# A macaron block on one core: weight rows in 1 MB loads by expert pairs n and n + 8, half of the sorted tiles' down matrices addressed on chip, sorted results added in place

## The chip, the cores and the metric

The kernel runs on one core of a Trainium2 chip. The metric is the device time of one execution in microseconds (us); the median of several runs is given, and one further execution was profiled. TensorE is written PE (its weight load PEld), VectorE DVE, ScalarE ACT, GpSimd POOL and SyncE SP, as in the profile.

## The reference

The input x has 8 batches of 1024 tokens with 128 features. Three stages follow each other, each on a layer norm of x and added to x: half of a mixture of experts, causal attention with one head of 128, and half of the same mixture again.

```python
x = x + 0.5 * ffn(layernorm(x))
x = x + attention(layernorm(x))
x = x + 0.5 * ffn(layernorm(x))

# ffn: 16 experts, 64 inner units each, the best 4 per token, and one shared expert
scores = sigmoid(xt @ gate_w.T)
_, idx = top_k(scores + gate_b, 4)
w = scores[idx] / sum(scores[idx]) * 2.5           # comb: w at idx, 0 elsewhere
y = sum over e of comb[:, e, None] * (silu_and_mul(xt @ w13[e].T) @ w2[e].T)
y = y + silu_and_mul(xt @ w13_s.T) @ w2_s.T
```

All is float32.

## The kernel before

**Units of work.** A batch is cut into 8 tiles of 128 tokens, and 4 tiles make a group of 512 (`GT` = 4, `W` = 512). There are 16 groups and two layers of experts, so 32 groups of expert work, done in two ways.

*Dense groups* (class `Group`, 20 of the 32). All 16 experts are computed for all tokens, two experts at a time: the 64 units of two experts fill 128 partitions, so there are `NP` = 8 steps k. Per step PE runs `gate` (L677) and `up` (L683), 128x512 each, ACT the silu (`gate_act`, L690), DVE the product (`units`, L694) into a buffer `hid`, then DVE or POOL multiplies it by the routing weights (`weigh`, L699), and PE adds it to the group's output in PSUM (`down`, L710, four matmuls of 128x128). The shared expert is a ninth term of that sum, and `add` puts it onto x.

The routing weights must lie along the free dimension, the same for all 64 units of an expert. So `store_weights` (L610) writes the transposed weights to DRAM (`cd`, 16 rows of 512), and `load_weights` (L619) reads them back, each row copied to 64 partitions, into buffers `cb`. Before, experts 2n and 2n + 1 form step n; a part has two steps, `CBP` = 4 parts make a group, and each part is loaded by two DMAs of 256 KB, one for either half of the partitions: 8 DMAs a group, 160 in all. Four buffers `cb` exist, so one group's weights.

*Sorted groups* (classes `SortedGroup`, `Chunk`, `Rows`, 12 of the 32, in three chunks of two batches, `CHUNKS`). Only the chosen experts are computed. `sort_steps` normalises, routes, adds the shared expert and puts x away in DRAM (`keep`, L847, into `kept`). `Chunk` numbers the 16 x 128 x 4 (token, expert) pairs by expert, padded to tiles of 128, 80 tiles in all; `scatter` (L1041) writes the normed rows to `rows` in DRAM by indirect DMA on POOL, 64 times a chunk. `rows` exists twice and is cleared to zero beforehand (`clear`, L1516, ten DMAs of 512 KB each). `Rows` then takes 8 tiles at a time as two halves h of 4: `load` (L1112) fetches rows, `turn` (L1143) transposes them on PE, `up` (L1154) multiplies by the expert's gate and up matrices, read from a table on chip at an offset in a register (`find_experts` loads four registers per half on PE), `gate_act`, `units` and `turn_units` (L1178) follow, and `down` (L1187) multiplies by the expert's down matrix: half h = 0 on partitions 0 to 63, half h = 1 on 64 to 127, side by side. The down matrices come from DRAM: `load_down` (L1130, L1136) reads eight offsets into SP's registers and issues eight DMAs of 32 KB into a buffer `wt`, of which there are two. `store` (L1200) writes the result rows. After the chunk, `gather_steps` fetches each tile of `kept` (L864, 64 KB) into a buffer `got`, gathers its four result rows per token by indirect DMA on POOL (L868), adds them with their weights on DVE (L877) and stores the tile (L885), to `kept` in the first layer, to the output in the second. In the first layer x is read again from `kept` later (L1561).

**What sets the order.** No scheduler of the compiler reorders anything: class `Plan` fixes the order of every engine's instructions at build time. Each step has an engine, an expected duration, a rank, the steps it follows, and buffers that it takes and frees. `Plan.run` advances a model clock per engine and each time emits the open step of lowest rank that can begin first. DMAs are issued by SP, whose queue is in order, except the indirect ones on POOL and a few on ACT. A DMA's landing is modelled by one line of transfers at 0.23 MB/us and 1.9 us. Eight semaphores, in turn, mark the landings of SP's and ACT's DMAs. `READY`, `EXPERTS` and so on are base ranks; in `expert_steps` the downs of group p rank at EXPERTS + p - 0.5, before the gates of group p and after those of p - 1.

## Time and profile before

| what | value |
|---|---|
| median of 3 runs | 925.82 us (921.67 to 927.11) |
| the profiled execution, its own time | 927.32 us |
| its span, first to last instruction | 925.5 us |
| mean granted PE clock | 0.987 |
| PE / DVE / POOL / ACT busy | 95% / 74% / 61% / 60% of the span |
| bytes moved by DMA | 139.52 MB, 151 GB/s on the mean |
| queue of SP's DMAs (q1) | 46.0% of 16 engines' span; POOL's indirect ones (q0) 9.7% |
| `cb` loads (L619) | 160 issues, 642 ns of SP each, 103 us together |
| `wt` loads (L1136) | 240 issues, 514 ns of SP each, 123 us together |

How to read it: "busy" is the time in which at least one instruction of the engine runs; "PEclk" and "DMA" are digits for 40 equal slices of the span, a digit being tenths (PEclk: of full speed; DMA: mean busy share of the core's 16 DMA engines). A wait row names the engine and instruction that waited, what ended the wait, and then the total in us, how often, and the longest. Instructions of SP carry the letter q: they issue, and the engine does nothing else. "PE" counts two records for one float32 matmul.

### The profile page before, as it was taken

What the parts mean: (1) busy time and instruction counts of PE and PEld (TensorE: products, weight loads), DVE (VectorE), ACT (ScalarE), POOL (GpSimd) and SP (SyncE); (2) the same over time, 40 slices, a digit from 0 to 9 for tenths busy, and PEclk for the clock granted to TensorE, in tenths of its full rate; (3) what the DMA queues carried; (4) which work ended last, traced back from release to release, by engine and by line L of the source; (5) the groups of instructions that cost most, each with busy time, mean ns of one, the idle gap of its engine ahead of it and who ended that gap; (6) DMA issues with size and microseconds to landing.
All of it is one profiled execution on the core that took longest, in us unless ns stands there. A gap on an engine that the chain in (4) does not pass through costs nothing.

```text
span 925.5 us, 17703 instructions
## 1 busy us (share of the span) xinstructions
PE 882.7 (95%) x5364; PEld 628.9 (68%) x5364; DVE 689.1 (74%) x2194; ACT 555.3 (60%) x1065; POOL 568.5 (61%) x597
## 2 busy tenths in 40 slices
PE   8899999989999999999899999999998989999998
PEld 5547576558587767778677676667576967666665
DVE  5767888848887776877577898687887646687875
ACT  6566644887875566776467567777657535334321
POOL 3442378887446788547475768887865672177560
PEclk9998999999999999999999999999999989999999
DMA  7979661144576844575566543142567567666671
GB/s 218 237 189 246 165 169 37 35 118 127 139 188 173 223 128 125 157 187 141 161 164 153 158 114 116 39 117 68 153 153 191 147 199 202 174 175 170 156 180 35
DMA packets 173694, 139.52 MB, mean 151 GB/s; under 512 B 17760, under 2 KB 144288, under 8 KB 173472
## 3 DMA queue, kind: packets, MB, share of 16 engines
q1 hardware_dynamic: 160032, 111.95, 46.0%
q0 software_dynamic: 12288, 25.19, 9.7%
q10 hardware_dynamic: 1280, 1.26, 0.4%
q8 instruction: 43, 0.70, 0.3%
q14 instruction: 51, 0.42, 0.1%
HBM read 90.49 MB, written 47.84 MB: 149 GB/s over the span
## 4 chain that ended last, share of the span: by engine, by line
PE 58%; POOL 19%; issue 7%; DMA 5%; ACT 4%; DVE 4%; SPq 1%; ACTq 0%; POOLq 0%; DVEq 0%
PE psum L710 13%; POOL rows L1041 12%; PE psum L677 9%; PE psum L683 9%; PE psum L1154 5%; DMA row<-rows 3%; PE psum L1434 3%; PE psum L1143 3%; PE psum L650 3%; PE psum L1187 2%; PE psum L1393 2%; POOL got L868 2%; PE psum L496 2%; PE psum L1421 1%; POOL mv_f L471 1%
## 5 line engine op out<-in xcount | busy, mean ns | idle before, releaser
L868 POOL DMA_INDIRECT got<-results,place x192 | 189.2, 985 | 99.5 <-issue 45.0
L1041 POOL DMA_INDIRECT rows<-xnc,place x192 | 194.8, 1014 | 75.5 <-issue 54.4
L710 PEld LDWEIGHTS psum<-wd,hid 128*128 128x128 f32 x1280 | 159.9, 194 | 33.1 <-issue 20.3
L710 PE MATMUL psum<-wd,hid 128*128 128x128 f32 x1280 | 168.3, 279 | 4.8 <-issue 2.5
L690 ACT ACTIVATE sg<-psum 128x512 f32<-128x512 f32 x160 | 94.5, 597 | 121.6 <-PE psum L677 98.9
L677 PE MATMUL psum<-hT,wg 128*128 128x512 f32 x320 | 164.7, 596 | 1.7 <-ACT sg L690 1.6
L683 PE MATMUL psum<-hT,wu 128*128 128x512 f32 x320 | 163.4, 592 | 0.0
L694 DVE TENSOR_TENSOR hid<-psum,sg 128x512 f32<-128x512 f32 x160 | 109.3, 688 | 56.5 <-PE psum L683 46.9
L683 PEld LDWEIGHTS psum<-hT,wu 128*128 128x128 f32 x320 | 60.8, 190 | 76.5 <-issue 71.5
L699 DVE TENSOR_TENSOR hid<-hid,cb 128x512 f32<-128x512 f32 x132 | 100.7, 770 | 3.0
L1434 PEld LDWEIGHTS psum<-v,prT 128*128 128x128 f32 x576 | 70.1, 192 | 14.3 <-issue 7.8
L1434 PE MATMUL psum<-v,prT 128*128 128x128 f32 x576 | 74.1, 278 | 1.8 <-DVE prT L1425 1.3
L1393 PE MATMUL psum<-k,q 128*128 128x512 f32 (+2 forms) x192 | 71.0, 504 | 3.9 <-POOL k L1310 3.5
L677 PEld LDWEIGHTS psum<-hT,wg 128*128 128x128 f32 x320 | 51.9, 191 | 26.3 <-issue 20.0
L877 DVE SCALAR_TENSOR_TENSOR got<-got,wk 128x128 f32<-128x128 f32 x192 | 65.2, 358 | 3.8 <-DMA got<-results,place 2.1
L1306 POOL TENSOR_TENSOR sg<-sg,cs 128x512 f32<-128x512 f32 x32 | 40.3, 1281 | 44.7 <-ACT sg L1296 44.5
L1154 PE MATMUL psum<-table,hTs 128*128 x480 | 64.3, 282 | 0.1
L1154 PEld LDWEIGHTS psum<-table,hTs 128*128 128x128 f32 x480 | 59.3, 195 | 5.6 <-issue 2.2
L455 DVE BATCH_NORM_STATS2 st<-x 128x6 f32<-128x128 f32 x192 | 53.2, 277 | 11.2 <-DMA x<-in_x 5.1
L1407 ACT ACTIVATE pr<-psum,top 128x128 f32<-128x128 f32 (+3 forms) x64 | 47.5, 745 | 12.1 <-DVE top L1402 11.7
L1425 ACT COPY prT<-psum 128x512 f32<-128x512 f32 (+3 forms) x85 | 37.2, 477 | 27.0 <-PE psum L1421 25.1
L1393 PEld LDWEIGHTS psum<-k,q 128*128 128x128 f32 x192 | 32.8, 196 | 26.3 <-issue 16.1
(148 smaller groups left out, 1515.5 us busy)
## 6 DMA issues: line engine op xcount, KB each, us to landing
cb<-cd SPq DMA_DIRECT2D x160, 256.0 KB
row<-rows SPq DMA_DIRECT2D x60, 256.0 KB
results<-row SPq DMA_DIRECT2D x60, 256.0 KB
rows<-sums SPq DMA_DIRECT2D x20, 512.0 KB
wt<-in_w_down SPq DMA_DIRECT2D x240, 32.0 KB
x<-in_x SPq DMA_DIRECT2D x16, 256.0 KB
kept<-x SPq DMA_DIRECT2D x12, 256.0 KB
rows<-xnc,place POOLq DMA_INDIRECT x192
```

The costliest lines, as they stand in the source:

```text
L677: nc.tensor.matmul(pair_of(("gu", self.id, k))[0], wg[:, k * P : (k + 1) * P], self.hT(), start=True, stop=True,)
L683: nc.tensor.matmul(pair_of(("gu", self.id, k))[1], wu[:, k * P : (k + 1) * P], self.hT(), start=True, stop=True,)
L690: nc.scalar.activation(buf("sg", a), pair_of(a)[0], AF.Silu)
L694: nc.vector.tensor_tensor(buf("hid", a), pair_of(a)[1], buf("sg", a), ALU.mult)
L699: engine.tensor_tensor(hid, hid, cb, ALU.mult)
L710: nc.tensor.matmul(y[:, cols], units[:, cols], wsd if k == NP else wd[:, k, :], start=(self.terms[part] == 1 and j == tiles[0]), stop=(sel ...
L868: nc.gpsimd.indirect_dma_start(out=buf("got", (self.id, j))[:, k, :], out_offset=None, in_=self.chunk.results, in_offset=bass.IndirectOffs ...
L877: nc.vector.scalar_tensor_tensor(got[:, TOPK, :], got[:, k, :], self.chunk.weight[:, self.n * GT + j, k : k + 1], got[:, TOPK, :], ALU.mul ...
L1041: nc.gpsimd.indirect_dma_start(out=row_views[self.n % 2][t * TOPK + k], out_offset=bass.IndirectOffsetOnAxis(ap=self.place[:, t, k : k + 1 ...
L1154: nc.tensor.matmul(p[:, cols], buf("hTs", (self.id, h))[:, cols], table[:, bass.ds(self.at[h][j], D)], start=True, stop=True,)
L1393: nc.tensor.matmul(s[:, c:e], q[:, i * P : self.width], k[:, c:e], start=True, stop=True)
L1434: nc.tensor.matmul(o, buf("prT", self.id)[:, j, :], buf("v", self.b)[:, j, :], start=(j == 0), stop=(j == i),)
```

## The change

- **Routing weights.** Expert n is paired with n + 8 instead of its neighbour, so step n holds experts n and n + 8 (the gate and up matrices are laid out that way by `paired` ahead of the launch, and `wd` is loaded in two halves). `CBP` is 2: a part has four steps, and since the rows of experts n to n + 3 now lie behind each other in `cd`, one DMA of 1 MB loads a part for all 128 partitions. Two buffers `cb` of twice the size.
- **Down matrices of sorted tiles.** A table `low` on partitions 0 to 63 holds the down matrices of all 16 experts (one DMA, `load_low`); half h = 0 of `Rows.down` reads it at the register offset that `up` has loaded. Half h = 1 still loads its four matrices per `Rows`, into the upper partitions of the same tensor, four buffers instead of two.
- **Sorted results.** `gather_steps` fetches a whole group from `kept` into a buffer of `x` (one DMA of 256 KB), adds the gathered rows there and stores the group with one DMA.
- **The planner.** SP's DMAs are modelled on eight lanes, each waiting for its own last landing; `pieces` says how many DMAs a step issues. `PATIENCE` is 3.0; downs rank at + 0.5, after the gates of their own group; early x loads begin at 30, the second clearing of `rows` at 160.
- **Buffers.** `un` and `hs` have one instead of two.

The diff, cut to its core:

```diff
                 work += self.SWITCH
-            self.free_at[e] = end = t + work
+            end = t + work
             if s.port:
                 self.port = end
+            if s.moves and e == "SP":
+                end = t
+                for _ in range(s.pieces):
+                    end = max(end, self.lanes[self.lane]) + work / s.pieces
+                    self.transfers = max(end + 0.5, self.transfers) + s.moves / s.pieces / self.RATE
+                    self.lanes[self.lane] = self.transfers + self.LAND
+                    self.lane = (self.lane + 1) % self.LANES
+            self.free_at[e] = end
             if s.moves:
-                self.transfers = max(end + 0.5, self.transfers) + s.moves / self.RATE
+                if e != "SP":
+                    self.transfers = max(end + 0.5, self.transfers) + s.moves / self.RATE
                 end = self.transfers + self.LAND
...
     CHUNKS = ((0, (4, 5)), (1, (0, 1)), (1, (2, 3)))
-    CBP = 4
+    CBP = 2
     CB = 2
...
         ("row", 4, [P, GT, D]),
-        ("got", 4, [P, TOPK + 1, D]),
-        ("wt", 2, [P, GT, D]),
-        ("un", 2, [P, W]),
-        ("hs", 2, [P, W]),
+        ("got", 4, [P, TOPK, D]),
+        ("un", 1, [P, W]),
+        ("hs", 1, [P, W]),
     ):
...
     wd = sbuf([P, NP, D], "wd")
-    nc.sync.dma_start(out=wd, in_=w_down.rearrange("(n p) d -> p n d", p=P))
+    for h in range(2):
+        nc.sync.dma_start(
+            out=wd[h * I : (h + 1) * I, :, :],
+            in_=w_down.rearrange("(h n i) d -> h i n d", h=2, i=I)[h],
+        )
     wsd = sbuf([P, D], "wsd")
...
     table = sbuf([P, E * D], "table")
+
+
+    low = sbuf([P, E * D], "low")
+    plan.pool("wt", E // GT)
+    buffers["wt"] = [tiles_of(low[:, m * GT * D : (m + 1) * GT * D]) for m in range(E // GT)]
     cs = sbuf([P, 2, S], "cs")
...
             )
-            self.pairs = cd.rearrange("(n h) s -> h n s", h=2)
+            self.pairs = cd.rearrange("(h n) s -> h (n s)", h=2)
...
             cb = buf("cb", (self.id, part))
-            for h in range(2):
-                nc.sync.dma_start(
-                    out=cb[h * I : (h + 1) * I, :, :],
-                    in_=self.pairs[h, part * N : (part + 1) * N, :].unsqueeze(0).broadcast_to([I, N, W]),
-                )
+            nc.sync.dma_start(
+                out=cb.rearrange("p n s -> p (n s)"),
+                in_=self.pairs[:, part * N * W : (part + 1) * N * W].unsqueeze(1).broadcast_to(
+                    [2, I, N * W]
+                ),
+            )
...
                     sp(
-                        2.0 / CBP, rank + 0.01 * m, lambda m=m: self.load_weights(m),
+                        0.6, rank + 0.01 * m, lambda m=m: self.load_weights(m),
                         after=[s, shared], take=[("cb", (n, m), NP // CBP)], moves=2.0 / CBP,
...
                         pe(
-                            0.89 * share, rank - 0.5 + 0.1 * part,
+                            0.89 * share, rank + 0.5 + 0.1 * part,
                             lambda k=k, part=part: self.down(part, k),
...
-        def fetch(self, j):
-            nc.sync.dma_start(out=buf("got", (self.id, j))[:, TOPK, :], in_=self.kept[:, j, :])
+        def fetch(self):
+            nc.sync.dma_start(out=x_of(self.b, self.g), in_=self.kept)
...
         def gathered(self, j, k):
-            got = buf("got", (self.id, j))
+            xt = x_of(self.b, self.g)[:, j, :]
             nc.vector.scalar_tensor_tensor(
-                got[:, TOPK, :], got[:, k, :], self.chunk.weight[:, self.n * GT + j, k : k + 1],
-                got[:, TOPK, :], ALU.mult, ALU.add,
-            )
-
-        def store_sorted(self, j):
-            t = self.g * GT + j
-            to = in_tiles(out, self.b, slice(t, t + 1)) if self.layer else self.kept[:, j : j + 1, :]
-            nc.sync.dma_start(out=to, in_=buf("got", (self.id, j))[:, TOPK : TOPK + 1, :])
+                xt, buf("got", (self.id, j))[:, k, :],
+                self.chunk.weight[:, self.n * GT + j, k : k + 1], xt, ALU.mult, ALU.add,
+            )
+
+        def store_sorted(self):
+            to = in_tiles(out, self.b, tiles_of_group(self.g)) if self.layer else self.kept
+            nc.sync.dma_start(out=to, in_=x_of(self.b, self.g))
         def gather_steps(self, rank, after):
+            fetched = sp(
+                0.5, rank, self.fetch, after=[*after, self.away], take=[("x", (self.b, self.g), 1)],
+                moves=0.25,
+            )
             ends = []
...
                 r = rank + 0.02 * j
-                before = [
-                    sp(
-                        0.5, r, lambda j=j: self.fetch(j), after=[*after, self.away],
-                        take=[("got", a, 1)], moves=0.064,
+                before = [fetched]
+                for k in range(TOPK):
+                    got = pool(
+                        1.27, r, lambda j=j, k=k: self.gather(j, k),
+                        after=[fetched] if k == 0 else [fetched, first],
+                        take=[("got", a, TOPK)] if k == 0 else [], moves=0.064,
                     )
-                ]
-                for k in range(TOPK):
-                    got = [
-                        pool(
-                            1.27, r, lambda j=j, k=k: self.gather(j, k),
-                            after=before if k == 0 else [*after, first], moves=0.064,
+                    first = got if k == 0 else first
+                    before = [
+                        dve(
+                            0.36, r, lambda j=j, k=k: self.gathered(j, k), after=[got, *before],
+                            free=[("got", a)], port=True,
                         )
                     ]
-                    first = got[0] if k == 0 else first
-                    before = [
-                        dve(
-                            0.36, r, lambda j=j, k=k: self.gathered(j, k), after=[*got, *before],
-                            port=True,
-                        )
-                    ]
-                ends.append(
-                    sp(
-                        0.5, r, lambda j=j: self.store_sorted(j), after=before, free=[("got", a)],
-                        moves=0.064,
-                    )
-                )
-            return ends
+                ends += before
+            return [
+                sp(
+                    0.5, rank, self.store_sorted, after=ends, free=[("x", (self.b, self.g))],
+                    moves=0.25,
+                )
+            ]
...
         def load_down(self):
-            w = buf("wt", self.id)
-            for h in range(2):
-                q = 2 * self.i + h
-                _, rows = nc.values_load_multi_w_load_instructions(
-                    self.chunk.owner[0:1, NS + q * GT : NS + (q + 1) * GT],
-                    engines=[mybir.EngineType.SP], min_val=0, max_val=(E - 1) * I,
-                    skip_runtime_bounds_check_because="the owner is held below the number of experts",
-                )
-                for j, row in enumerate(rows):
-                    nc.sync.dma_start(
-                        out=w[h * I : (h + 1) * I, j, :], in_=w_down[bass.ds(row, I), :]
-                    )
+            q = 2 * self.i + 1
+            _, rows = nc.values_load_multi_w_load_instructions(
+                self.chunk.owner[0:1, NS + q * GT : NS + (q + 1) * GT],
+                engines=[mybir.EngineType.SP], min_val=0, max_val=(E - 1) * I,
+                skip_runtime_bounds_check_because="the owner is held below the number of experts",
+            )
+            for j, row in enumerate(rows):
+                nc.sync.dma_start(
+                    out=buf("wt", self.id)[I:, j, :], in_=w_down[bass.ds(row, I), :]
+                )
...
                         bank_of(("xd", self.id, h))[:, cols], buf("hs", self.id)[rows, cols],
-                        buf("wt", self.id)[rows, j, :],
+                        buf("wt", self.id)[rows, j, :] if h else low[rows, bass.ds(self.at[0][j], D)],
                         start=True, stop=True, tile_position=(h * I, 0),
...
                 3.0, rank, self.load_down, after=[owner, *in_front], take=[("wt", n, 1)],
-                moves=0.25,
+                moves=0.125, pieces=GT,
             )
...
+    def load_low():
+        nc.sync.dma_start(
+            out=low[:I, :].rearrange("i (e c) -> i e c", e=E),
+            in_=w_down.rearrange("(e i) c -> i e c", i=I),
+        )
+
     have_table = chain(
-        sp, READY, [given(100.0)], *[(0.5, lambda n=n: load_table(n)) for n in range(2)], moves=1.0
+        sp, READY, [given(100.0)], *[(0.5, lambda n=n: load_table(n)) for n in range(2)],
+        (0.5, load_low), moves=1.5,
     )
...
-    cleared = [given(40.0)]
     rows_free = []
...
             chain(
-                sp, SORT + 900, cleared,
+                sp, SORT + 900, [given(40.0 + 120.0 * m)],
                 *[(0.5, lambda m=m, part=part: clear(10 * m + part, 20)) for part in range(10)],
-                moves=5.2,
+                moves=5.2, pieces=10,
             )
...
+    def paired(w):
+
+        return w.reshape(2, E // 2, I, D).transpose(1, 0, 2, 3).reshape(E * I, D)
+
     w_qkv = np.stack(
...
         "gate_b": np.asarray(L0_ffn_gate_b).reshape(1, E),
-        "w_gate": transposed(w13[:, :I].reshape(E * I, D)),
-        "w_up": transposed(w13[:, I:].reshape(E * I, D)),
+        "w_gate": transposed(paired(w13[:, :I])),
+        "w_up": transposed(paired(w13[:, I:])),
         "w_sh": transposed(L0_ffn_w13_s),
```

More of the change, by code (lines that the diff above doesn't have):

```diff
@@ L50 @@
     SWITCH = 1.3
-    PATIENCE = 2.0
+    PATIENCE = 3.0
+    LANES = 8
     RATE, LAND = 0.23, 1.9
@@ L60, in __init__ @@
         self.transfers = begin
+        self.lanes, self.lane = [begin] * self.LANES, 0
         self.port = begin
@@ L72, in add @@
     def add(self, engine, work, rank, emit, after=(), take=(), free=(), table=None, moves=0,
-            port=False):
+            port=False, pieces=1):
         s = Step(engine, work, rank, emit, take, free, table, moves, port)
+        s.pieces = pieces
         for a in after:
@@ L1549 @@
                 for g in range(NG):
-                    s = load_steps(b, g, READY + 2.5, [given(20.0)], lambda b=b, g=g: load_x(b, g))
+                    s = load_steps(b, g, READY + 2.5, [given(30.0)], lambda b=b, g=g: load_x(b, g))
                     begins["f0", b, g] = [stats_steps("f0", b, g, READY + 2.5, [s])]
```

## The prediction

> **What bounds the kernel now.** I read the page's first two parts, then the busy time by stretch, then TensorE's waits, then SyncE's timeline ahead of the worst of them, and last the DMA view. The median is 925.82 us; the profiled execution took 927.32 us with a span of 925.5, so 1.8 us lie outside the span. Sums below are made against 925.5; what lies outside and the 1.5 us by which this execution is above the median cancel.
>
> ```profile
> span 925.5 us, 17703 instructions
> PE 882.7 (95%) x5364; PEld 628.9 (68%) x5364; DVE 689.1 (74%) x2194; ACT 555.3 (60%) x1065; POOL 568.5 (61%) x597
> ...
> PEclk9998999999999999999999999999999989999999
> DMA  7979661144576844575566543142567567666671
> ...
> DMA packets 173694, 139.52 MB, mean 151 GB/s; under 512 B 17760, under 2 KB 144288, under 8 KB 173472
> ```
>
> TensorE has 95%, and the clock dips below full in few slices. How much could be won? The two programs hold the same matmuls. Sixteen records of L1154, each half of an f32 matmul over 128 columns, took 1.79 us back to back, 0.112 us each; counting all columns of the program at that pitch (transposes once, row-group pairs side by side) gives 851.7 us of pure TensorE work, an estimate. So 74 us of the span are waits, refills, slow clock, head and tail. No change that leaves the matmuls alone wins more.
>
> ```profile
> 0.00:190.00 190.00, 176.53 (x898) 115.20 (x898) 142.91 (x543) 116.41 (x223) 105.04 (x131) 0.97 0.59 159
> 190.00:800.00 610.00, 585.16 (x3856) 435.40 (x3856) 453.82 (x1429) 400.40 (x779) 399.31 (x403) 0.99 0.56 149
> 800.00:925.50 125.50, 121.04 (x613) 78.29 (x612) 92.39 (x222) 38.50 (x63) 64.16 (x64) 1.00 0.58 145
> ```
>
> Columns: stretch, length, busy PE, PEld, DVE, ACT, POOL, clock, DMA share (mean of 16 engines), GB/s. The last stretch, dense groups only, is full.
>
> ```profile
> PE psum L1143 <- DMA row<-rows: 10.5, 8, 3.3
> PE psum L1421 <- ACT pr L1407: 4.7, 5, 1.4
> PE psum L496 <- DVE q L1299: 3.5, 2, 3.0
> PE psum L1393 <- POOL k L1310: 3.5, 3, 1.7
> PE psum L710 <- issue: 2.5, 1, 2.5
> PE psum L710 <- DVE hid L699: 2.3, 3, 1.1
> ```
>
> The largest wait is for sorted rows (total us, times, longest). Its cause is SyncE's queue, here before the 3.27 us stall that ends at 753.2:
>
> ```profile
> 743.43 6.07 SPq L1136 DMA_DIRECT2D wt<-in_w_down  x8
> 749.54 1.14 SPq L1112 DMA_DIRECT2D row<-rows  x2
> ```
>
> Eight down-matrix loads take SyncE 6 us, and the rows stand behind them. The clock view by stretch shows 0.86 for 750 to 775, against 1.00 around it, so a long stall is paid about twice.
>
> ```profile
> q1 hardware_dynamic: 160032, 111.95, 46.0%
> ...
> cb<-cd SPq DMA_DIRECT2D x160, 256.0 KB
> ```
>
> **The change, part by part.** Orders and counts are of the built programs, durations of the trace.
>
> *Down matrices.* Of 240 loads 120 go, and 30 of 60 owner reads: 120 x (514 + 38 + 30 ns) + 30 x 366 ns = 81 us of SyncE. A row load then stands behind four loads, about 3 us, not 6. But the new order leaves less room too: TensorE work between the last thing that a row load waits for and its transpose falls from 12.7 to 12.2 us in the middle case, and from 7.6 to 5.7 at worst, while landings behind the observed stalls took 3 to 7 us. I take 8 of the 10.5 us, and 3 of the slow clock: -11 (0 to -15). In exchange TensorE gets 120 register operations; in L1154 such operations of 37 ns run ahead while matmuls keep their 0.112 us pitch, so 0, and 4.4 us if none were covered. The one load of the table `low` (512 KB) goes in near 100 us, 100 us ahead of its use.
>
> *Gathers into x.* 48 fetches and 48 stores become 12 and 12: 72 x 0.45 = 32 us less on SyncE. A fetch now waits for a free x buffer; GpSimd's gathers queue behind it and the x loads of later batches compete. 0 (-3 to +10).
>
> *Order.* Downs rank after the gates of their own group: matmuls that wait for anything fall from 1003 to 926, those with under 3 us of TensorE work between cause and wait from 430 to 343. -3 (-8 to +5). Moving the second clearing of `rows` (15.6 us of SyncE at 71.1, DMA share 1.04 in 80 to 90) and the early x loads: -2 (-5 to +2). One buffer each of `un`, `hs`: +1 (0 to +5); eight more ACT table loads of 1.28 us lie in ACT's 40% idle time, and 14 weighings moved from POOL to DVE (10 us) in DVE's 26%. `wd` in halves: one more issue at the start, 0.
>
> These parts together: **-15 us** (-25 to +15).
>
> *Weights in one load per half group.* 160 loads of 256 KB become 40 of 1 MB: 160 x 0.642 = 103 us of SyncE become about 26. The bytes are the same. What differs is the shape: before, the source's outermost dimension is 64 copies and the destination's 64 partitions; now the source's is 2 (experts n and n + 8), then 64 copies of 2048 values, against 128 partitions. First the row. The count of packets under 512 B shows how many engines a load uses: each engine ends its share with a 4-byte packet. 710 hardware and 384 indirect DMAs x 16 = 17,504, and the gate's loads have 256 packets of 64 B: 17,760, exactly the page's figure. So today every DMA runs on all 16 engines; but no DMA of this trace has an outermost dimension below 64, so it can't tell what 2 does. Packets of 8192 B are seen once, in the rope load: 312 ns at best (26 GB/s). By this, 128 packets on 16 engines are 8 x 0.312 = 2.5 us per 1 MB, better than now (2048-byte packets at 126 ns: 4.0 us), and the sum is 925 - 15 = 910.
>
> Against it stands the Trainium skill, DMA: Bandwidth & Descriptors, section "Why a DMA increments its semaphore by 16 and not by 1": the number of engines is the largest up to 16 that divides the size of the slowest dimension (other than 1) on both sides. For 2 and 128 that is **two engines**. Then a 1 MB load is 64 packets per engine x 0.312 = 20.0 us, plus landing, and both halves of a group use the same two. The rule agrees with all 1094 DMAs here (64 and 128 give 16), and the exception that the section names is for GpSimd's queue. I take the rule.
>
> What that makes of the time: everything else that is spread over 16 engines also sends a sixteenth through those two, in order behind the weights. By stretch of before, I add the weight loads (in 1 MB: 8, 23.3 and 8.7, from the 32, 93 and 35 issues) at 20.0 us and one engine's share of all other packets at their measured durations:
> - 0 to 190: first load at 26, then 160 + 56 - 19 (second clearing, moved on), ends at 223, against 190: +33.
> - 190 to 800: 466 + 249 (161 for 512-byte packets less 14 for the down matrices, 64 for gathers and scatters, 19 for the clearing, 19 for the rest) = 715 against 610: +105.
> - 800 to the end: 175 + 36 = 211 against 125: +86, as the tail after the last load is in both.
>
> Sum +224. This supposes that the two engines are never idle. They are: a half's buffer is refilled only when its four experts are weighed, and a weighing that waits holds VectorE's whole queue, so the products behind it don't free their PSUM banks and the next gates stop TensorE; a row load behind a weight load lands up to 20 us later, with 6 to 12 us of room; and each DMA waits for the eighth before it (eight semaphores in turn), which holds SyncE. For that I add 8% of 715 in the middle, 57 us (0 to 170). Then 925 - 15 + 224 + 57 = 1191, **1190 us**. TensorE's waits are then some 340 us, most at downs and at row transposes; the slow clock costs nothing more, since TensorE isn't what ends last.
>
> **Rivals.**
> - *All 16 engines (17%).* The loads spread whatever their outermost dimension. For it: 1094 of 1094 DMAs did. Against: none had a small one. Then 910 (895 to 935), faster than before. It decides between four and eight engines: with eight, two halves take 10 us of the 21 us that a group has in the last stretch; with four 20 us, which with 6 us of other packets is too much.
> - *Two engines, but mostly hidden (8%).* Loads are issued early: room from issue to weighing is 20 to 70 us of TensorE work in the middle. If nothing else is held up there, only the last stretch (21 us per group against 40) and half of the first pay: 910 + 86 + 17 = 1013. Against it: SyncE issues in order and other loads share the engines.
> - *Two engines and every load's delay handed to TensorE in turn (10%).* If row loads and weights alternate without overlap, the middle's 23 loads each stall by 20 less 8 us of room: 276 in place of the 57, some 1410.
> - *The register read is not covered*, at most +4 in any case.
>
> **How the numbers follow.** Two engines as computed 65%, hidden 8%, in turn 10%, all engines 17%. The prediction is the likeliest's, 1190, whose own range is 1090 to 1340. The range for 8 in 10 takes in most of both two-engine rivals and leaves out all engines: 1020 to 1400. Faster by over 1%: 0.12, from all engines with its gain kept; within 1% (what a measurement of this kernel can tell from no change): 0.04; slower: 0.84, the 83% and a little of the 17%.
>
> **What would show it.** Packets under 512 B: (400 + 384) x 16 + 256 = 12,800 if all use 16 engines, 40 x 14 fewer, 12,240, with two. With two: the weighing (L720) waits for `cb` over and over, row transposes (L1159) wait longer in total than 10.5 us, the last stretch grows most per group (near 40 us each), and the mean DMA share falls below 0.5 while TensorE falls to about 75%. A span under 935 with 12,800 such packets proves the rule wrong for this shape; 12,240 with a span under 1000 proves the queueing wrong.

## The result, and the profile after

The changed kernel takes 1350.76 us (median of 4 runs, 1349.03 to 1353.44) against 926.19 us for the kernel before (921.67 to 927.11, 4 runs): a ratio of 1.460 (95% interval 1.4546 to 1.4656), 46% slower. Seven of the runs below (experiments 5 to 9, "on a slower chip") met chips on which the kernel before itself took 1163 to 1165 us in place of 923 to 926; from them ratios, differences between runs on such chips, and the order of things in the trace are used.

The page of the changed kernel, with the lines that answer to those shown of before and, last, the shares of the chain that ended last, by engine and by line:

```profile
span 1347.9 us, 16990 instructions
PE 946.6 (70%) x5364; PEld 672.8 (50%) x5364; DVE 684.0 (51%) x2196; ACT 572.8 (42%) x1085; POOL 541.6 (40%) x583
...
PEclk9687789879697978959777877999879778878887
DMA  4161141251113324424233432212227432422221
...
DMA packets 140009, 136.06 MB, mean 101 GB/s; under 512 B 12240, under 2 KB 123920, under 8 KB 134672
...
DMA 60%; PE 24%; DVE 5%; issue 5%; POOL 4%; SPq 2%; ACT 1%; ACTq 0%; DVEq 0%; POOLq 0%
DMA cb<-cd 41%; DMA row<-rows 9%; PE psum L731 4%; DMA results<-row 4%; PE psum L1450 2%; PE psum L698 2%; PE psum L704 2%; PE psum L1170 2%; POOL rows L1059 2%; DMA cd<-cT 2%; DMA x<-kept 2%; PE psum L1409 2%; PE psum L1159 2%; PE psum L1203 1%; DVE hid L715 1%
```

The same shares by engine before:

```profile
PE 58%; POOL 19%; issue 7%; DMA 5%; ACT 4%; DVE 4%; SPq 1%; ACTq 0%; POOLq 0%; DVEq 0%
```

Read the packet count first: 12,240 under 512 B is the figure that was set down for two engines, (360 x 16 + 40 x 2) + 384 x 16 + 256. The packets' times agree: wherever weight loads run, 1.75 to 2.02 of their packets are under way on the mean. TensorE has fallen from 95% to 70%, and the DMA row, a mean over 16 engines, is *lower* than before, although DMA has gone from 5% to 60% of the chain, 41% on the weight loads alone. A mean over 16 can't show that two of them are full: a digit of 1 is what two busy engines out of 16 give.

Where the waits are (what waited, what ended it, total us, times, longest):

```profile
DVE hid L720 <- DMA cb<-cd: 321.3, 27, 17.5
...
PE psum L1159 <- DMA row<-rows: 147.3, 10, 30.8
...
POOL hid L720 <- DMA cb<-cd: 100.4, 4, 39.0
```

Weighing (L720) waits for weights on both engines that do it, and TensorE's wait for sorted rows has gone from 10.5 us to 147.3. Before, the weighing had this one wait for weights:

```profile
POOL hid L699 <- DMA cb<-cd: 15.8, 1, 15.8
```

By stretch, cut at three places that both programs have: the fourth dense group's add (168.5 us before, 243.8 after), the last down of a sorted tile (801.1 and 1138.6) and the end (925.5 and 1347.9). The columns are those of the stretches in the prediction (stretch, length, busy PE, PEld, DVE, ACT, POOL, clock, DMA share, GB/s). Before, then after:

```profile
0.00:168.50 168.50, 158.42 (x826) 105.07 (x827) 128.94 (x489) 96.67 (x188) 87.34 (x111) 0.97 0.65 174
168.50:801.10 632.60, 604.38 (x3944) 446.51 (x3942) 468.74 (x1486) 420.14 (x814) 417.00 (x423) 0.99 0.54 146
801.10:925.50 124.40, 119.94 (x598) 77.31 (x596) 91.45 (x221) 38.50 (x63) 64.16 (x64) 1.00 0.58 146
```

```profile
0.00:243.80 243.80, 169.31 (x862) 114.96 (x863) 136.38 (x502) 110.06 (x211) 65.61 (x89) 0.86 0.32 99
243.80:1138.60 894.80, 640.95 (x3940) 471.38 (x3939) 464.41 (x1496) 427.53 (x817) 415.51 (x430) 0.85 0.33 105
1138.60:1347.90 209.30, 136.29 (x567) 86.42 (x565) 83.22 (x199) 35.20 (x58) 60.48 (x64) 0.81 0.26 87
```

The three grew by 75, 262 and 85 us. The trace's packets give the load of the two engines in each: half of the time of all weight packets (8192 bytes, mean 322 ns) plus a sixteenth of all other packet time.

| stretch | weights on each of the two | all else | sum | length | not in use |
|---|---|---|---|---|---|
| to the landing of the eighth load, 231.7 | 163 | 55 | 218 | 231.7 | 14 |
| 243.8 to 1138.6 | 478 | 237 | 715 | 894.8 | 180 |
| 1138.6 to 1347.9 | 173 | 33 | 206 | 209.3 | 3 |

The sums are estimates: packets overlap a little, for in the four groups from 1158.3 to 1333.1 the same sum gives 183.5 us in 174.8. In the first stretch (whose first load begins at 28.1 us) and in the last the two engines are as good as full, and they set the time. In the middle they are not: some 180 us are missing. Where those went is read from a table of stretches again, with the borders set at the first and last packet of weight loads. The first, third and fifth line have no weight load under way, the others have two, one behind the other:

```profile
410.00:462.00 52.00, 46.01 (x318) 36.68 (x319) 38.09 (x162) 32.94 (x65) 13.26 (x14) 0.91 0.32 95
462.00:508.30 46.30, 27.10 (x134) 16.41 (x132) 13.08 (x33) 16.48 (x30) 17.67 (x19) 0.81 0.28 101
508.30:556.00 47.70, 45.35 (x340) 35.88 (x341) 35.85 (x131) 35.15 (x69) 35.38 (x39) 0.93 0.51 149
556.00:600.00 44.00, 14.58 (x83) 9.67 (x81) 11.55 (x20) 10.40 (x21) 24.53 (x24) 0.69 0.28 103
600.00:633.70 33.70, 32.32 (x217) 25.16 (x218) 21.74 (x75) 22.01 (x40) 9.01 (x10) 0.90 0.39 117
633.70:679.80 46.10, 19.46 (x165) 15.57 (x163) 18.14 (x88) 12.65 (x22) 16.02 (x18) 0.76 0.29 96
...
890.80:937.00 46.20, 44.54 (x251) 31.29 (x250) 36.37 (x114) 34.85 (x67) 38.41 (x40) 1.00 0.22 82
```

The middle **alternates in large part**. In the first six lines TensorE (the second figure after the border) is busy 46.0 of 52.0, 45.4 of 47.7 and 32.3 of 33.7 us without loads: it is the bound. With loads it has 27.1 of 46.3, 14.6 of 44.0 and 19.5 of 46.1: the two engines are. It isn't so everywhere: in the last line loads run and TensorE is busy 44.5 of 46.2 us. Over the whole middle, weight packets are under way for 522 us, and TensorE is busy for 309 of them (59%); in the other 373 us it is busy for 332 (89%). So the two kinds of work overlap only in part, and the time is longer than either.

The loads also go out late: the buffers of the group loaded at 553 were free from about 523 on, but its routing weights were stored to `cd` at 544; the next group's first buffer was free from about 582 on, its load went out at 632. The fourth line is the worst case, and SyncE's timeline inside it says how a sorted tile gets into it:

```profile
553.10 1.68 SPq L638 DMA_DIRECT2D cb<-cd  x2
554.88 20.90 SPq L1130 DMA_DIRECT2D row<-rows  x1
575.88 11.23 SPq L630 DMA_DIRECT2D cd<-cT  x1
```

Both halves of a group are issued at 553 to 555, right ahead of a row load. That one issue then holds SyncE for 20.9 us, about as long as the first weight load runs (556.0 to 578.6). The row lands behind the second (578.6 to 600.0), and TensorE, which had run dry at 570.6, goes on at 601.4: its wait of 30.8 us. The next thing in the queue, the store of another group's weights to `cd`, is late as well. This is no single case: SyncE's 392 issues took 733 us together, fifty of them over 3 us each (511 us in all); the 702 of before took 396. Over the nine row waits above 3 us the times from the end of the issue to use fall in two kinds: four rows were issued 18 to 26 us ahead of their transposes and landed late; five were issued only 3 to 6 us ahead, since SyncE was late.

### The profile page after: what moved, and what is told of

Its sections match the earlier page's. It is cut to its first block, busy times and chain, and to the rows that moved or that the text cites. A ratio compares the mean times of both kernels' runs of the same rounds, so it can differ in the third digit from the quotient of the medians.

```text
span 1347.9 us, 16990 instructions
## 1 busy us (share of the span) xinstructions
PE 946.6 (70%) x5364; PEld 672.8 (50%) x5364; DVE 684.0 (51%) x2196; ACT 572.8 (42%) x1085; POOL 541.6 (40%) x583
## 2 busy tenths in 40 slices
DMA packets 140009, 136.06 MB, mean 101 GB/s; under 512 B 12240, under 2 KB 123920, under 8 KB 134672
## 3 DMA queue, kind: packets, MB, share of 16 engines
q1 hardware_dynamic: 126352, 108.52, 24.9%
## 4 chain that ended last, share of the span: by engine, by line
DMA 60%; PE 24%; DVE 5%; issue 5%; POOL 4%; SPq 2%; ACT 1%; ACTq 0%; DVEq 0%; POOLq 0%
DMA cb<-cd 41%; DMA row<-rows 9%; PE psum L731 4%; DMA results<-row 4%; PE psum L1450 2%; PE psum L698 2%; PE psum L704 2%; PE psum L1170 2%; POOL rows L1059 2%; DMA cd<-cT 2%; DMA x<-kept 2%; PE psum L1409 2%; PE psum L1159 2%; PE psum L1203 1%; DVE hid L715 1%
## 5 line engine op out<-in xcount | busy, mean ns | idle before, releaser
L720 DVE TENSOR_TENSOR hid<-hid,cb 128x512 f32<-128x512 f32 x146 | 104.4, 728 | 324.0 <-DMA cb<-cd 321.3
L731 PE MATMUL psum<-wd,hid 128*128 128x128 f32 x1280 | 186.0, 301 | 100.7 <-DVE hid L720 51.6
L731 PEld LDWEIGHTS psum<-wd,hid 128*128 128x128 f32 x1280 | 176.8, 216 | 115.3 <-DVE hid L720 53.2
L704 PE MATMUL psum<-hT,wu 128*128 128x512 f32 x320 | 176.8, 636 | 53.5 <-DVE hid L715 53.4
L698 PE MATMUL psum<-hT,wg 128*128 128x512 f32 x320 | 178.5, 642 | 0.0
L1159 PE MATMUL psum<-ident,row 128*128 128x128 f32 x240 | 43.1, 314 | 149.5 <-DMA row<-rows 147.3
L1159 PEld LDWEIGHTS psum<-ident,row 128*128 128x128 f32 x240 | 31.8, 160 | 158.7 <-DMA row<-rows 65.9
L698 PEld LDWEIGHTS psum<-hT,wg 128*128 128x128 f32 x320 | 58.4, 208 | 40.0 <-issue 35.8
L898 DVE SCALAR_TENSOR_TENSOR x<-got,wk,x 128x128 f32<-128x128 f32 x192 | 63.6, 347 | 13.1 <-DMA got<-results,place 11.0
L720 POOL TENSOR_TENSOR hid<-hid,cb 128x512 f32<-128x512 f32 x14 | 19.4, 1400 | 125.7 <-DMA cb<-cd 100.4
L1163 ACT COPY hTs<-psum 128x512 f32<-128x512 f32 x50 | 29.2, 589 | 89.8 <-PE psum L1159 88.6
```

The lines of the kernel that those rows point to most:

```text
L698: nc.tensor.matmul(pair_of(("gu", self.id, k))[0], wg[:, k * P : (k + 1) * P], self.hT(), start=True, stop=True,)
L704: nc.tensor.matmul(pair_of(("gu", self.id, k))[1], wu[:, k * P : (k + 1) * P], self.hT(), start=True, stop=True,)
L720: engine.tensor_tensor(hid, hid, cb, ALU.mult)
L731: nc.tensor.matmul(y[:, cols], units[:, cols], wsd if k == NP else wd[:, k, :], start=(self.terms[part] == 1 and j == tiles[0]), stop=(sel ...
L1159: nc.tensor.transpose(pt[:, j, :], buf("row", (self.id, h))[:, j, :], ident)
```

## The experiments

**1. The same kernel, with 64 outermost in the weight loads.** One load per half group becomes two of 512 KB, each of one row of `pairs` copied to 64 partitions. Bytes, buffers, order and the rest of the change stay.

```diff
-            nc.sync.dma_start(
-                out=cb.rearrange("p n s -> p (n s)"),
-                in_=self.pairs[:, part * N * W : (part + 1) * N * W].unsqueeze(1).broadcast_to(
-                    [2, I, N * W]
-                ),
-            )
+            for h in range(2):
+                nc.sync.dma_start(
+                    out=cb[h * I : (h + 1) * I, :, :].rearrange("p n s -> p (n s)"),
+                    in_=self.pairs[h : h + 1, part * N * W : (part + 1) * N * W].broadcast_to(
+                        [I, N * W]
+                    ),
+                )
```

> The changed kernel, with its order, costs and buffers kept, but each 1 MB weight load split into two of 512 KB whose outermost dimension is 64 copies on both sides. If the two engines are the cause: all engines again, packets under 512 B (440 + 384) x 16 + 256 = 13,440, packets of 8192 B spread over 16 engines (a load about 1.3 us of each), and the 910 us of the forecast without the weights' part (895 to 935); TensorE's wait for sorted rows under 5 us. If instead the new order, the single buffers or the coarse parts (four steps wait for one part) cost the time: above 1200.

Measured: 907.5 us (906.82 to 909.38) against 922.8 for the kernel before beside it, ratio 0.984 (0.9792 to 0.9888). From its page:

```profile
span 905.0 us, 17054 instructions
PE 872.5 (96%) x5364; PEld 623.9 (69%) x5364; DVE 693.1 (77%) x2196; ACT 572.1 (63%) x1085; POOL 555.6 (61%) x583
...
DMA packets 141209, 136.06 MB, mean 150 GB/s; under 512 B 13440, under 2 KB 125120, under 8 KB 135872
...
cb<-cd SPq DMA_DIRECT2D x80, 512.0 KB
```

13,440 is (440 + 384) x 16 + 256: every DMA on 16 engines. Forty more DMAs, and 443 us less. The whole loss sits in the shape of one load, and this version is faster than the kernel before, by 15 us.

**2. The kernel before, with the weights part alone** (`CBP` 2, experts n and n + 8, the one load of 1 MB, `wd` in two halves).

```diff
-    CBP = 4
+    CBP = 2
...
-            self.pairs = cd.rearrange("(n h) s -> h n s", h=2)
+            self.pairs = cd.rearrange("(h n) s -> h (n s)", h=2)
```

> The kernel before with the weights' part of the change alone: experts paired n with n + 8, two parts of 1 MB in one load each. If two engines are the cause, this alone makes the time: 1250 to 1450, likeliest 1360, and packets under 512 B fall by (160 - 40 - 1) x 16 + 40 x 14 = 2,464 to 15,296. If the planner's order or the gathers in x cause it: 926 to 950.

Measured: 1441.95 us (1441.29 to 1444.73), ratio 1.563 (1.5558 to 1.571), 15,296 short packets as expected. The weights part alone costs 519 us; the rest of the change, worth 15 us with good loads, takes 91 us off that. SyncE's two longest waits here point at what it removes: the fetch of a single sorted tile, behind the store of one from `got`, and the down-matrix loads (L1141), behind the landing of weight loads:

```profile
SPq L869 <- DMA out_x<-got: 185.0, 11, 23.1
SPq L1141 <- DMA cb<-cd: 135.4, 12, 16.3
```

The changed kernel has no fetch or store of single tiles and half the down-matrix loads. How the 91 us divide between these two wasn't tested. TensorE's row waits are 140.0 us in all, near the 147.3 of the full change, so the row waits come with the weights part.

**3 and 4. Four and eight engines.** The routing weights are stored two or four times per half (`COPIES` 2, as shown, or 4), so that the load's outermost dimension is 4 or 8; the 1 MB and the one load stay.

```diff
-    next_cd = turns("cd", 4, [E, W], dram)
+    COPIES = 2
+    next_cd = turns("cd", 4, [COPIES * E, W], dram)
...
-                    [2, I, N * W]
+                    [2 * COPIES, I // COPIES, N * W]
```

> The changed kernel, but the routing weights are written to DRAM twice for each half (four stores of 16 KB in place of one of 32), so that the load's outermost dimension is 4: four engines by the rule. A 1 MB load is then 32 packets of 8192 B per engine, 32 x 0.309 = 9.9 us in place of 20. Two engines as cause: 930 to 1000, likeliest 955, the weighing waits for its weights some 30 us in total in place of 420, packets under 512 B (460 + 384) x 16 + 256 - 40 x 12 = 13,280. If the number of engines does not matter but the order does: 1350 as before.

> As with four engines, but four copies for each half (eight stores of 16 KB in place of one of 32 KB, about 3.5 us more of SyncE per group): outermost dimension 8, a load 16 x 0.309 = 4.9 us. Two engines as cause: 905 to 935, likeliest 915, below or at the kernel before; packets under 512 B (540 + 384) x 16 + 256 - 40 x 8 = 14,720. If the order is the cause: 1350.

Measured: 1096.92 us with four (1086.21 to 1107.04), ratio 1.192 (1.1823 to 1.2021); 965.67 us with eight (958.46 to 970.68), ratio 1.045 (1.0373 to 1.0528). Both were expected too fast. The packet line and the weighings of either page, four first:

```profile
DMA packets 142329, 136.72 MB, mean 126 GB/s; under 512 B 13280, under 2 KB 126240, under 8 KB 136992
...
L725 DVE TENSOR_TENSOR hid<-hid,cb 128x512 f32<-128x512 f32 x146 | 103.1, 719 | 118.6 <-DMA cb<-cd 115.8
```

```profile
DMA packets 146330, 138.04 MB, mean 143 GB/s; under 512 B 14720, under 2 KB 130240, under 8 KB 140992
...
L725 DVE TENSOR_TENSOR hid<-hid,cb 128x512 f32<-128x512 f32 x146 | 103.7, 723 | 67.3 <-DMA cb<-cd 64.5
```

The counts are exact for four, (420 x 16 + 40 x 4) + 6400, and for eight, (500 x 16 + 40 x 8) + 6400, where 6400 is 384 x 16 + 256. With experiment 1 and the changed kernel this is a row of doses (packet time is the mean of a run's 8192-byte packets; a load is packets per engine times it; the last column counts SyncE's issues that held it for over 3 us, and their sum):

| engines per load | packets each | packet | a load | time | above the first | weighing on DVE waits | row waits | SyncE held |
|---|---|---|---|---|---|---|---|---|
| 16 | 8 | 560 ns | 4.5 us | 907.5 us | | none listed | 0.2 us | 2, 9 us |
| 8 | 16 | 520 ns | 8.3 us | 965.7 us | +58 | 64.5 us | 24.9 us | 10, 58 us |
| 4 | 32 | 387 ns | 12.4 us | 1096.9 us | +189 | 115.8 us | 73.2 us | 26, 171 us |
| 2 | 64 | 322 ns | 20.6 us | 1350.8 us | +443 | 321.3 us | 147.3 us | 50, 511 us |

From 16 engines to eight a us of load costs 58 / 3.8 = 15 us of time, from there on (189 - 58) / 4.1 = 32 (30 by the two quicker runs of four engines) and (443 - 189) / 8.2 = 31, with 40 loads. With eight engines a group's two loads need 17 us of the 21 us that a dense group takes, and the same sum as above leaves the eight engines unused for 219 of the 656 us of the middle; yet 34 of the 58 us are lost there. So a bound by occupied engines isn't all of it: below eight engines it is as if three in four loads handed on all that they are longer by.

**5. A control for 3 and 4: all eight copies' stores, but loads on 16 engines** (as in experiment 1, from the first copy). On a slower chip.

```diff
-                    in_=self.pairs[h : h + 1, part * N * W : (part + 1) * N * W].broadcast_to(
-                        [I, N * W]
-                    ),
+                    in_=self.pairs[
+                        h * COPIES : h * COPIES + 1, part * N * W : (part + 1) * N * W
+                    ].broadcast_to([I, N * W]),
```

> Control for the four- and eight-engine kernels: the eight stores of 16 KB per group are kept, but the load takes the first copy in two DMAs with 64 outermost, on all engines. If the stores cost little: 907 to 917. If they are what made the eight-engine kernel 58 us slower than the kernel with 64 outermost: near 966.

Measured: 1121.65 us where before took 1163.46, ratio 0.968 (0.9589 to 0.9769). The expectation in us can't be held against that; but with the stores of the eight-engine kernel this one is faster than before, not slower, and VectorE's weighings wait 0.4 us for weights in place of 64.5. The stores are not what cost in 3 and 4.

**6. The weight loads issued by ScalarE**, still on two engines: does SyncE's queue or do the engines delay the rows? Tried twice, both on slower chips.

```diff
-            nc.sync.dma_start(
+            nc.scalar.dma_start(
                 out=cb.rearrange("p n s -> p (n s)"),
```

> The changed kernel with two engines per weight load, but these 40 loads are issued by ScalarE, on a queue of its own; nothing else moves. If the sorted rows wait because they stand behind the weights in SyncE's queue on the same two engines: TensorE's wait for rows falls from 147 us to under 40, the time to 1150 to 1300, likeliest 1230. If the weights' own latency (weighing waits 420 us) carries the loss: 1320 to 1400, rows or not. ScalarE waits for free weight buffers here, which may add some 20 us.

> The changed kernel with its 40 weight loads issued by ScalarE, still two engines each, told before where the kernel before itself took 1163 us. If the two engines (whatever the queue) delay the row loads, the row waits stay above 70 us and the time is within 1300 to 1400 us; if SyncE's own queue was what delayed them, row waits fall below 40 us and the time below 1250.

Measured: 1405.58 and 1404.83 us, ratios 1.2135 (1.2008 to 1.2262) and 1.207 (1.2013 to 1.2131). TensorE's row waits, second try:

```profile
PE psum L1159 <- DMA row<-rows: 83.9, 10, 31.3
```

More telling is the order in the trace: all seven row waits above 3 us are now for rows issued 11 to 25 us ahead of their transposes; none was issued late. So the rows seem to stand in the engines behind the weights, whichever queue those came from; in the changed kernel SyncE's own lateness comes on top in five of nine. In the second try SyncE's 352 issues take 306 us, 14 of them over 3 us each (121 us together), so most of that holding goes with weight loads in its own queue. Whether ScalarE's queue is the better place in us is open, since the changed kernel itself was not timed on such a chip.

**7. The planner told the truth.** The order was made for loads of 4.4 us (1 MB at the modelled 0.23 MB/us); here it is made for 20. Still two engines. Tried twice, both on slower chips.

```diff
-                        after=[s, shared], take=[("cb", (n, m), NP // CBP)], moves=2.0 / CBP,
+                        after=[s, shared], take=[("cb", (n, m), NP // CBP)], moves=4.6,
```

> The changed kernel with two engines per weight load, but the planner is told their real length: the modelled transfer of a load becomes 20 us (4.6 in place of 1.0 in the step's megabytes), so every engine's order is made for it. Same loads, same two buffers. If the loss beyond the sum of the two engines' work comes from an order made for loads of 4.4 us: 1130 to 1220, likeliest 1170, near that sum. If the two buffers bound it whatever the order: above 1300.

> The changed kernel, still two engines, with the planner told that a weight load takes 20 us (moves of 4.6 MB), told before where the kernel before itself took 1163 us. If the order made for 4.4 us is most of the loss, 1150 to 1220 us; if two engines with two buffers can't do better in any order, 1300 or more, with the waits moved from the row transposes to the downs of the dense groups.

Measured: 1488.04 and 1482.33 us, ratios 1.285 and 1.272 (1.2648 to 1.2791). The row waits for DMA are gone from the list; in their place TensorE's largest wait, second try, is at the downs of dense groups:

```profile
PE psum L731 <- DVE hid L720: 137.3, 24, 15.5
```

The order made for slow loads moves the wait from the rows to the weighings. The theory that the order is most of the loss would have had 1150 to 1220 us; it isn't supported: on such a chip the time is 318 us above before, and 77.5 us above the variant of experiment 6 beside it. What the changed kernel takes there isn't known, so how much the order gives or costs is open. More than two `cb` buffers, with which loads could go out earlier, were not tried.

**8 and 9. Which of the small parts made the 15 us?** Experiment 1 with all eight down matrices loaded again, and with the downs ahead of the gates again. Both on a slower chip.

```diff
-                        buf("wt", self.id)[rows, j, :] if h else low[rows, bass.ds(self.at[0][j], D)],
+                        buf("wt", self.id)[rows, j, :],
```

```diff
-                            0.89 * share, rank + 0.5 + 0.1 * part,
+                            0.89 * share, rank - 0.5 + 0.1 * part,
```

> The kernel with 64 outermost (907.5 us), but all eight down matrices of every `Rows` loaded from DRAM again (240 loads, two buffers, no table on chip). What it costs over 907.5 is what the register read is worth. The prediction's term of 11 us (0 to 15) gives 918, with a row wait of 5 to 10 us back; if the register read is worth nothing, 907 (904 to 910).

> The kernel with 64 outermost (907.5 us), but with the downs ranked at - 0.5 again, ahead of the gates of their own group. The prediction's term of 3 us (-5 to 8) gives 911 (903 to 916); if the order is what pays in that kernel, 918 or more, with longer waits of TensorE for products of VectorE.

Measured: 1194.6 us, ratio 1.027 (1.0228 to 1.0309), and 1177.14 us, ratio 1.012 (1.0076 to 1.0164). What differs on these chips shows in ScalarE's waits of the second; "remote" is a releaser that the trace can't name, and experiment 1 has none on this list:

```profile
ACT prT L1442 <- remote: 46.6, 7, 14.6
ACT row L1211 <- remote: 35.5, 4, 16.4
```

All such rows of ScalarE make 181 us. With these stalls in the kernel, TensorE waits for ScalarE, and terms of 3 and 11 us can't be read against 907.5. Beside experiment 5 (on another such chip, and the same kernel as experiment 1 but for the copies it stores: ratio 0.968) these two are 73 and 55.5 us slower, so there both parts seem worth far more than that. On an ordinary chip neither was measured: the split of the 15 us stays open.

**10. The changed kernel again**, meant as the control for 6 and 7.

> The changed kernel itself, as the control for the two runs with ScalarE's ring and with the planner told, if it meets a chip where the kernel before takes 1160 us. If ScalarE's ring or the other order help or harm there by more than the chip does, this one differs from them: 1290 to 1330 us if ScalarE's ring makes nothing better, above 1440 if it does, and row waits near 147 us if the ring is what brought them to 84. If ScalarE's ring changes nothing, 1395 to 1415 us with row waits of 75 to 95. If the chip is one where the kernel before takes 923 us, 1351 us again.

Measured: 1346.57 us against 923.86, ratio 1.459 (1.4542 to 1.4637), row waits 146.7 us. The chip was one of the ordinary ones, so it repeats the result and is no control.

## Why the prediction was right, and where its terms were not

- **The number of engines: right.** It was the step on which all hung, and the trace of before could not show it. The Trainium skill's rule (DMA: Bandwidth & Descriptors, "Why a DMA increments its semaphore by 16 and not by 1") gave two, and here the counts with outermost 2, 4, 8 and 64 agree with it to the packet: 12,240, 13,280, 14,720 and 13,440. The rows of before (all DMAs on 16 engines) spoke for 910 us only because no row there had a small outermost dimension.
- **20.0 us per load: right**, 20.6 from the packets. But the price for 16 engines, 8 x 0.312 = 2.5 us, was wrong by the same row: in the changed shape a packet takes 560 ns with 16 engines at it, a load 4.5 us. The duration was the best packet of the rope load; that whole load of 1 MB took 4.0 us in the trace of before, and this was the figure to take.
- **The first stretch, +33:** the eighth load landed at 231.7 us, where the sum had 223. The two engines were nearly full from the first load's start, as assumed. The growth of 75 at the fourth group's add is larger than 33 + 9 since in before that add lies at 168.5, not at the border of 190 (21.5 us), and since 12 us pass from the landing to the add.
- **The last stretch, +86: right**, +85, at 43.7 us a group ((1333.1 - 1158.3) / 4) where 40 was foreseen.
- **The middle: the load of the two engines is right, the idle time is the term that failed.** The sum was 715 us (466 + 249); the trace has 715 (478 + 237). Left unused are 180 us. The step that failed is "For that I add 8% of 715 in the middle, 57 us (0 to 170)": 8% was a guess for a full pipe with small gaps, and the measured value is just outside its bounds; what happens is that TensorE-bound and DMA-bound stretches alternate in large part. That is the mechanism of the rival "in turn" at about two thirds of its 276 us, and 1350.8 lies nearer to its 1410 than to 1190. It is also what the doses say: at eight engines there is no lack of engine time, and 58 us are lost all the same. Why the loads do not overlap better is not settled: what an order made for their length gives stayed open (experiment 7), and more buffers were not tried.
- **SyncE's queue: held, but by more than was named.** The prediction has SyncE held by the wait for the eighth DMA before, and counted on 77 us less of SyncE's issuing from the merged loads. The issues themselves became longer: 733 us in place of 396. What this costs by itself wasn't separated.
- **"The slow clock costs nothing more": wrong in the middle,** in a size that isn't separated. Stretches without loads, where TensorE is the bound, ran at a clock of 0.90 to 0.93 in the table above. In the middle TensorE's busy time rose from 604.4 to 641.0 us for as good as the same matmuls, so some 37 us at most.
- **The other parts, -15: right with good loads** (907.5 against 922.8), though the split into 11, 3 and 2 wasn't shown. With slow loads they were worth 91 us, not 15: costs were added that don't add. By itself the weights part costs 519 us, where the sum gave it 224 + 57 = 281. That the whole fell within 1020 to 1400 is therefore in part luck: with only 15 us off, 1442 would have become 1427. It lies 11 us above the likeliest case's own range, 1090 to 1340.
- **The threshold, "between four and eight engines": wrong.** It used 5 us per load at eight; packets of 520 ns make it 8.3, and the handing on does the rest. Eight still loses 4.5%; of the doses tried, only 16 wins.

All in all the forecast of 1190 was 161 us low: 138 of it in the middle (895 against 715 + 57 - 15 = 757), of which 123 are the idle term (180 against 57) and 15 the saving that was taken off there, and 21 in the first stretch (243.8 against 223); the last was 2 us below its sum, and the rest lies outside the span.

## What to carry to other kernels

Ahead of merging loads, look at the outermost dimension of both sides of the new one: two loads of 512 KB with 64 outermost took 4.5 us of each of their engines, the one load of 1 MB with 2 outermost 20.6 us, and that made a kernel 443 us slower that was 15 us faster without it. Here, with loads slow on few engines, the mean DMA share fell (0.57 to 0.32) instead of rising; count the packets below 512 B, and look for stretches in which the compute engine and the transfers take turns, because there neither one's occupancy gives the total. Where an order was made beforehand for short loads, the engine time of longer ones is a floor and not the price: 715 us of it became 895 in the middle.

## What the runs showed of the hardware that was not expected

- Packets of 8192 B took longer the more engines shared a load: medians of 309, 318, 520 and 593 ns with 2, 4, 8 and 16 engines, that is about 51, 85, 126 and 234 GB/s (from the means in the table). Whether that comes from the engines reading the same few rows of DRAM, or from their number, wasn't told apart. The rope load of before, 128 different rows on 16 engines, took 312 to 352 ns a packet and 1 MB in 4.0 us, which speaks for the rows, but it is one load, with ten packets under way on the mean.
- Issues on SyncE became longer with the weight loads in its queue: 1.87 us each on the mean against 0.56 before and 0.59 with 64 outermost; during 49 of the 50 that held it for over 3 us, weight packets were under way. The longest, a row load's right behind two weight loads, took 20.9 us in a stretch with a mean DMA share of 0.28. The trace doesn't name what held it; it ended about when the first of the two loads did (575.8 and 578.6). ScalarE's issues did not become so long when it issued the loads: 48 took 24 us.
- A load on two engines delays loads that are spread over 16, also when it comes from another engine's queue: rows issued 11 to 25 us ahead of use were still late with the weights on ScalarE's.
